# Four-layer hybrid on one core: the end of layer 0 image by image, and a new order of work ahead of layer 3's recurrence

## The chip, the cores and the metric

The kernel runs on one core of a Trainium2 chip. Its time is device microseconds for one execution, from the start of the program to its end. Five engines take part: TensorE (PE, matmuls; its weight loads are shown apart as PEld), VectorE (DVE), ScalarE (ACT), GpSimd (POOL) and SyncE (SP, which here only issues transfers). Each works through its own queue in order, and an instruction at the head of a queue that waits holds back what stands behind it. All arithmetic is fp32. In the trace an fp32 matmul leaves two rows; the text calls such a row a record.

## What is computed

Four layers act on x with 4 images, 256 channels and 32 x 32 positions (1024 tokens an image, 4096 in all). The parts that the change touches, cut from the reference:

```python
# end of layer 0: gate, root-mean-square norm, projection, excitation
y = y * silu(z)
y = y * rsqrt(mean(y * y, axis=-1, keepdims=True) + EPS) * rms_w
out = einsum('bld,ed->ble', y, out_w)
out_img = out.reshape(b, h, w, c).transpose(0, 3, 1, 2)
pooled = mean(out_img, axis=(2, 3))
hdn = relu(pooled @ se1_w.T + se1_b)
attn = sigmoid(hdn @ se2_w.T + se2_b)
x = x + out_img * attn[:, :, None, None]
# layer 3, attention (feature is the layer norm of the tokens t)
QK = einsum('bnd,kde->bkne', feature, W_qk) + b_qk[None, :, None, :]
value = einsum('bnd,de->bne', feature, W_v) + b_v
query, key = QK[:, 0], QK[:, 1]
lam = einsum('bnd,bne->bde', softmax(key, axis=1), value)
mean = mean(lam, axis=(0, 2)); var = var(lam, axis=(0, 2))
bn = (lam - mean) * rsqrt(var + BN_EPS) * gamma + beta
t = t + einsum('bnd,bde->bne', query, bn)
# layer 3, recurrence over the 1024 tokens, again on a layer norm of t
i, f, o = sigmoid(x_t @ U + h @ V + b)   # each with its own U, V, b
g = tanh(x_t @ U_c + h @ V_c + b_c)
c_new = h * c + i * g
h = o * tanh(c_new)
```

(In the recurrence the cell takes h * c, so the gate f is not needed, and the kernel computes three gates of 256 columns.) Layer 0 is a Mamba-like scan ahead of the lines shown, layer 1 a non-local block whose 1x1 products run over channels, layer 2 softmax attention and a mixture of eight experts, two for each token.

## The kernel before

Sizes: P = 128 partitions, C = 2 channel chunks of 128, D = 256, B = 4 images, W = 512 tokens a block, TPB = 4 token tiles a block, TPI = 8 tiles an image, NT = 32 tiles in all, BPI = 2 blocks an image. The program is unrolled; a scheduler places instructions by their data, and `_in_order` pins the order as written for the engines PE, DVE and ACT over a stretch of the program.

End of layer 0. `_scan` (L376) goes through 8 steps of tokens and in each through the 4 images: transposes and products on TensorE, an exponential on ScalarE, masking and sums on VectorE, and at the end of each tile the gate, which writes the gated rows `zs` (L436). When all 32 tiles are there, `_out_and_se` (L439) lets ScalarE square each and sum it (L449), takes a square root (L451) and a reciprocal (L452). Then for each of 8 blocks VectorE rescales four tiles by row (L459), TensorE transposes them into `pt` (L463), VectorE copies these to `yT` times `rms_w` (L464), TensorE multiplies by `w_out` into `po` (L470), and ScalarE copies that to `o` and sums it for the mean (L473). After the last block come the mean (L478), two small products with a relu (L484, L486) and, for each chunk, a third product (L489), the sigmoid `att` (L491) and four updates of x (L493). Layer 1 starts with 1x1 products over x by halves (L535). ScalarE's transfer queue loads weights: those of layer 2 behind the last sigmoid here.

`_rsqrt` (L971) is 1/sqrt by an integer first guess and four Newton steps of three VectorE operations (L990 to L994); the recurrence has a copy of it (L1517 to L1539).

Layer 3, attention (`_layer3_attention`, L1247). The experts' outputs lie in DRAM as two rows for each token. For each image and each half of it, SP loads both as `y_in` (L1282; three buffers, each freed by the addition), GpSimd adds the two (L1285), VectorE adds them to the tokens (L1287) and takes statistics (L1291, L1292). For the image follow `_rsqrt`, a shift (L1297) and eight normalised `rows` by ScalarE (L1302); TensorE transposes these into channels (L1268) and VectorE copies them to `u` (L1273). Then the keys (L1318), their copy, maximum and exponential (L1323 to L1333), transposes of these (L1343, copied at L1345 as `kt`) and of u (L1347, L1353), values (L1357) and `lam` (L1361). BatchNorm over lam follows for each chunk (L621 to L627, with a square root at L625) and an affine pass in two operations (L1377, L1378). lam is then multiplied by the query weights for every image: `p_q` (L1384), copied by ScalarE to `lam_q` (L1389), and with the query bias `p_b` (L1394), copied to `add_col` (L1398).

Layer 3, recurrence (`_layer3_lstm`, L1401). It starts with loads of `b_l`, `w_u` and `w_v` on ScalarE's queue and small constants (L1429 to L1443). `ahead(n)` is a generator that makes what batch n of 128 tokens an image needs: `attended(n)` multiplies u by `lam_q` (L1464) and adds it to x (L1458); `input_gates(n)` takes means (L1501), centred rows (L1487), squares (L1493), variances (L1511), 1/sqrt, a product that spreads it over rows (L1545), products with `w_u` (L1560) and gates `xg` (L1571). It yields after each instruction or so: False after a product, True after one of the small operations on VectorE. For n = 0 all of it runs ahead of the recurrence; for n = 1 to 7 one part is taken in each step of the batch before:

```python
        for _ in ahead(0):
            pass
        start = len(nc.cur_bb.bb.instructions)
        inputs(0)
        for t in range(L):
```

Its products share two PSUM buffers named `beside`. A step is: the gates' inputs (L1607), 48 products of the hidden state (L1616), transposes on VectorE (L1645), activations (L1646, L1659), the cell's scan (L1652) and the new hidden state (L1661), which is stored over x's old place. Sums to the output (`added`, L1585, L1586) follow batch by batch.

## Time and profile before

| what | value | from |
|---|---|---|
| median of 3 runs | 3514.43 us (3514.23 to 3514.61) | times |
| profiled execution | 3514.67 us | times |
| span of that execution | 3512.7 us | page |
| mean granted clock of TensorE | 0.969 | times |
| last gated row of the scan ends | 295.4 us | timeline |
| layer 1's first products end | 372.2 us | timeline |
| last expert row scattered | 1386.6 us | timeline |
| last lam summed | 1528.2 us | timeline |
| first product of the hidden state | 1582.9 us | timeline |

The span is the profiled execution's time between its first and its last instruction on the device; the 2.0 us between it and the execution's time lie around it. Times of the trace count from the span's start. The page's slices are 3512.7 / 40 = 87.8 us each. A group's line in the timeline reads: start in us, busy time, engine, line, operation, output<-inputs, shapes and count; in square brackets the idle time ahead of it and what ended that. A group's busy time is the sum over its instructions, which need not follow each other without gaps. In the chain of waits a line reads: time, length, engine, what, line.

### The profile page before, as it was taken

How to read it: one execution, taken by the hardware profiler on the slowest of the kernel's cores; microseconds unless marked ns; L12 is line 12 of the kernel's file. 1: busy time of each engine (PE TensorE's matmuls, PEld its weight loads, DVE VectorE, ACT ScalarE, POOL GpSimd, SP SyncE). 2: the span in 40 equal slices, each digit the busy share in tenths (PEclk: the TensorE clock that was granted, in tenths of full speed). 3: DMA queues.
4: the chain of work that ended last, by engine and by line, in shares of the span. 5: the costliest groups of instructions: out<-in, count | busy, mean ns of one | idle time of the engine just before them, and what ended most of it. 6: DMA issues, size and time to landing. Idle time of an engine off the chain costs nothing.

```text
span 3512.7 us, 146893 instructions
## 1 busy us (share of the span) xinstructions
PE 3227.6 (92%) x65412; PEld 2536.4 (72%) x65412; DVE 2016.5 (57%) x8382; ACT 1245.0 (35%) x5047; POOL 416.3 (12%) x498
## 2 busy tenths in 40 slices
PE   7786899998999997789999999999999999999888
PEld 4464344447788886468888888888888888888776
DVE  5795534452211111747777776777777777767666
ACT  4623222223222222413334344343343343433333
POOL 0182001122433332100000000000000000000000
PEclk9898899999999999899999999999999999999999
DMA  1290001115556554100000000000000000000000
GB/s 67 80 303 5 9 0 37 37 50 197 195 189 219 208 190 165 60 2 4 4 11 4 5 10 4 4 10 4 6 9 5 10 4 5 10 4 5 10 4 10
DMA packets 79355, 189.31 MB, mean 54 GB/s; under 512 B 6592, under 2 KB 64256, under 8 KB 73728
## 3 DMA queue, kind: packets, MB, share of 16 engines
q0 software_dynamic: 16176, 116.06, 9.0%
q1 hardware_dynamic: 60624, 59.12, 5.7%
q8 instruction: 511, 8.37, 1.0%
q10 hardware_dynamic: 1920, 4.74, 0.4%
q14 instruction: 124, 1.02, 0.1%
HBM read 118.88 MB, written 61.02 MB: 51 GB/s over the span
## 4 chain that ended last, share of the span: by engine, by line
PE 41%; DVE 9%; ACT 4%; issue 2%; ACTq 0%; DVEq 0%
PE p_c L1616 11%; DVE turned L1645 7%; PE p_c L1607 7%; PE p_i L1607 4%; PE p_o L1607 4%; PE p_i L1616 4%; PE p_o L1616 4%; PE beside L1560 4%; ACT a_o L1646 2%; DVE x L1661 2%; ACT th L1659 2%; PE beside L1464 1%; PE beside L1501 0%; PE var L1511 0%; PE p_q L1384 0%
## 5 line engine op out<-in xcount | busy, mean ns | idle before, releaser
L1646 ACT ACTIVATE add<-turned 128x8 f32<-128x8 f32 x1024 | 214.3, 209 | 1027.5 <-DVE turned L1645 1027.5
L1616 PE MATMUL p_c<-w_v,x 128*4 128x64 f32 x16368 | 416.0, 219 | 72.8 <-DVE x L1661 71.0
L1607 PE MATMUL p_c<-xg,shift 128*128 128x64 f32 x2048 | 445.7, 299 | 0.0
L1616 PE MATMUL p_o<-w_v,x 128*4 128x64 f32 x16368 | 416.6, 219 | 0.1
L1616 PE MATMUL p_i<-w_v,x 128*4 128x64 f32 x16368 | 416.5, 219 | 0.0
L1607 PE MATMUL p_i<-xg,shift 128*128 128x64 f32 x2048 | 406.8, 280 | 0.0
L1645 DVE STREAM_TRANSPOSE turned<-p_c 128x64 f32<-128x64 f32 x1024 | 255.9, 250 | 257.1 <-PE p_c L1616 226.7
L1607 PE MATMUL p_o<-xg,shift 128*128 128x64 f32 x2048 | 396.0, 275 | 0.0
L1607 PEld LDWEIGHTS p_c<-xg,shift 128*128 128x128 f32 x2048 | 304.7, 188 | 117.6 <-issue 0.3
L1616 PEld LDWEIGHTS p_c<-w_v,x 128*4 128x4 f32 x16368 | 227.2, 85 | 196.3 <-DVE x L1661 121.2
L1661 DVE TENSOR_TENSOR x<-a_o,th 128x8 f32<-128x8 f32 x1024 | 171.9, 168 | 245.4 <-ACT th L1659 245.4
L1607 PEld LDWEIGHTS p_o<-xg,shift 128*128 128x128 f32 x2048 | 310.9, 192 | 0.3
L1607 PEld LDWEIGHTS p_i<-xg,shift 128*128 128x128 f32 x2048 | 304.8, 188 | 0.4 <-issue 0.3
L1187 PE MATMUL ph<-uT,w 128*128 128x256 f32 x1248 | 284.6, 386 | 20.8 <-DVE uT L1172 20.7
L1191 ACT ACTIVATE hT<-ph,w 128x256 f32<-128x256 f32 x312 | 147.9, 474 | 395.2 <-PE ph L1187 394.8
L1187 PEld LDWEIGHTS ph<-uT,w 128*128 128x128 f32 x1248 | 240.4, 194 | 58.2 <-DVE uT L1172 24.6
L1201 PE MATMUL po<-w,hT 128*128 128x256 f32 x1248 | 282.1, 379 | 0.0
L1616 PEld LDWEIGHTS p_o<-w_v,x 128*4 128x4 f32 x16368 | 281.2, 87 | 0.3 <-issue 0.3
L1616 PEld LDWEIGHTS p_i<-w_v,x 128*4 128x4 f32 x16368 | 281.2, 87 | 0.3
L1645 DVE STREAM_TRANSPOSE turned<-p_i 128x64 f32<-128x64 f32 x1024 | 271.6, 265 | 0.7 <-PE p_i L1607 0.3
L1645 DVE STREAM_TRANSPOSE turned<-p_o 128x64 f32<-128x64 f32 x1024 | 256.0, 250 | 0.3 <-PE p_o L1616 0.3
L1201 PEld LDWEIGHTS po<-w,hT 128*128 128x128 f32 x1248 | 234.0, 190 | 30.2
(437 smaller groups left out, 4395.4 us busy)
## 6 DMA issues: line engine op xcount, KB each, us to landing
sorted<-zeros SPq DMA_DIRECT2D x32, 1032.0 KB, 14.4
y_in<-results SPq DMA_DIRECT2D x16, 512.0 KB, 5.3
x<-in_x_dram SPq DMA_DIRECT2D x8, 512.0 KB, 8.7
tokens<-rows SPq DMA_DIRECT2D x4, 1024.0 KB, 4.7
x<-tokens SPq DMA_DIRECT2D x8, 512.0 KB, 4.2
out_dram<-x_l SPq DMA_DIRECT2D x64, 64.0 KB, 1.7
results<-y,place POOLq DMA_INDIRECT x78, 4.4
w_l<-in_w_l_dram ACTq DMA_DIRECT2D x1, 1092.0 KB, 11.4
```

Of the source, the lines that this page charges most:

```text
L1187: nc.tensor.matmul(ph, w1[:, k, bass.ts(n, P)], uT[:, k, :], start=k == 0, stop=k == C - 1,)
L1191: nc.scalar.activation(hT[:, n, :], ph, AF.Gelu, bias=b1[:, n : n + 1])
L1201: nc.tensor.matmul(po, hT[:, n, bass.ts(a, P)], w2[:, n, :], start=n == 0, stop=n == NHC - 1,)
L1464: nc.tensor.matmul(p, lam[:, k, b, bass.ts(m, P)], u_l3[:, k, b * L + n * SB : b * L + (n + 1) * SB], start=k == 0, stop=k == C - 1,)
L1560: nc.tensor.matmul(p[bass.ts(i, R), :], rows[:, k, bass.ts(g, R)], w_u[:, k, at : at + GQ // GC], start=k == 0, stop=k == C - 1, tile_posi ...
L1607: nc.tensor.matmul(p[:, :H], shift[:, row * B : row * B + P], xg[n][:, g, bass.ts(i, H)], start=True, stop=t == 0,)
L1616: nc.tensor.matmul(p[R * i : R * i + B, :H], hs[:, t - 1, bass.ts(k, B)], w_v[:, k, i * GQ + g * H : i * GQ + (g + 1) * H], start=False, s ...
L1645: nc.vector.transpose(zt.rearrange("p c w -> p (c w)"), pz[g][:, :H])
L1646: nc.scalar.activation(dst.rearrange("p (c b) -> p c b", c=C), zt[:, :, :B], f)
L1659: nc.scalar.activation(th, cell[:, :, 1], AF.Tanh)
L1661: nc.vector.tensor_mul(h, a_o, th)
```

## The change

It has five parts.

First, the end of layer 0. The square of each gated tile is issued in `_scan` right behind the gate, into column c*B + b (token step c, image b). `_out_and_se` multiplies `rms_w` into the projection's weights once (`wo`), takes 1/sqrt by `_rsqrt` on VectorE, first for the 28 columns of the first seven steps and then for the last four, and goes image by image. For an image it rescales eight tiles, in turn on VectorE and ScalarE, transposes them, and lets ScalarE copy them to `yT` and sum them there. The mean over tokens is taken of yT, ahead of the projection, and goes through the projection as one column: `pooled`, `p1` and `p2` are products with one column each, in the fixed order on TensorE between the four `project(m, i)`. The projection stays in four PSUM banks, and x is updated from there in four operations an image.

Second, `_rsqrt` and the recurrence's copy of it take three Newton steps.

Third, the attention of layer 3. The two expert rows are added by VectorE one after the other, GpSimd adds nothing. Image 0 is normalised half by half, with PE, DVE and ACT in the order written for this stretch, and the additions of images 1 to 3 are put behind image 0's last copy to u (`later`, an order on VectorE without a semaphore).

Fourth, `_lstm_constants`: the loads of `b_l` and the small constants are issued ahead of the attention instead of behind it.

Fifth, lam's products. A fourth block of `w_l3` holds the query weights the other way round, and the attention ends with `q`, the queries of the first 128 tokens of each image. BatchNorm's affine pass is one operation with a scale and an offset; a square root with an output named `none`, which nothing reads, is issued ahead of BatchNorm. `attended(0)` multiplies `q` by the normalised lam itself. The products that were `p_q` and `p_b` become `queries()`, a generator of eight groups of eight records; `ahead(0)` takes a group from it at given parts, five among the products behind attended(0) and the others at every fourth small operation, with TensorE's order fixed up to the last group.

```diff
-NW = {"w_l0": 260 + 512 + 256 + 64, "w_l2": 768 + 8, "w_l3": 768, "w_u": 768, "w_v": 768}
+NW = {"w_l0": 260 + 512 + 256 + 64, "w_l2": 768 + 8, "w_l3": 1024, "w_u": 768, "w_v": 768}
...
+                sq = pool.tile([P, D], F32, name="sq")
+                nc.scalar.activation(sq, zs[:, n, :], AF.Square, accum_out=ss[:, c * B + b : c * B + b + 1])
...
+        ps = ctx.enter_context(tc.tile_pool(name="out_ps", bufs=3, space=PSUM))
...
+        wo = keep.tile([P, C, D], F32, name="wo")
+        for k in range(C):
+            nc.vector.tensor_scalar_mul(
+                wo[:, k, :], w_out[:, k, :], s.col["rms_w"][:, k : k + 1]
+            )
+        for t in (slice(0, NT - B), slice(NT - B, NT)):
+            nc.vector.tensor_scalar_mul(ms[:, t], ss[:, t], 1.0 / D)
+            for _ in _rsqrt(s, pool, rstd[:, t], ms[:, t]):
+                pass
+        for b in range(B):
+            for i in range(BPI):
+                for j in range(i * TPB, (i + 1) * TPB):
+                    n = b * TPI + j
+                    r = rstd[:, j * B + b : j * B + b + 1]
+                    if j % 2:
+                        nc.scalar.mul(y[:, n, :], y[:, n, :], r)
+                    else:
+                        nc.vector.tensor_scalar_mul(y[:, n, :], y[:, n, :], r)
+                for k in range(C):
+                    pt = ps.tile([P, TPB, P], F32, name="pt")
+                    for j in range(TPB):
+                        nc.tensor.transpose(
+                            pt[:, j, :], y[:, b * TPI + i * TPB + j, bass.ts(k, P)], s.ident
+                        )
+                    nc.scalar.activation(
+                        yT[:, k, bass.ts(i, W)], pt.rearrange("p j q -> p (j q)"), AF.Identity,
+                        accum_out=part[:, k, i : i + 1],
+                    )
+            mean = pool.tile([P, C], F32, name="mean")
+            nc.vector.tensor_reduce(mean, part, AX.X, ALU.add)
+            nc.vector.tensor_scalar_mul(mean, mean, 1.0 / L)
+            pooled, p1, p2 = small[:, b, :C], small[:NSE, b, C : C + 1], small[:, b, C + 1 :]
+            def project(m, i):
+                for k in range(C):
+                    nc.tensor.matmul(
+                        o[m][i], wo[:, k, bass.ts(m, P)], yT[:, k, bass.ts(i, W)],
+                        start=k == 0, stop=k == C - 1,
+                    )
+            start = len(nc.cur_bb.bb.instructions)
+            project(0, 0)
+            for m in range(C):
+                for k in range(C):
+                    nc.tensor.matmul(
+                        pooled[:, m : m + 1], wo[:, k, bass.ts(m, P)], mean[:, k : k + 1],
+                        start=k == 0, stop=k == C - 1,
+                    )
+            pooled_s = pool.tile([P, C], F32, name="pooled")
+            nc.vector.tensor_copy(pooled_s, pooled)
+            project(0, 1)
             for k in range(C):
+                nc.tensor.matmul(
+                    p1, w_se1[:, k, :], pooled_s[:, k : k + 1], start=k == 0, stop=k == C - 1
+                )
+            hdn = pool.tile([NSE, 1], F32, name="hdn")
+            nc.vector.tensor_scalar(hdn, p1, s.col["se1_b"][:NSE], 0.0, ALU.add, ALU.max)
+            project(1, 0)
+            for m in range(C):
+                nc.tensor.matmul(
+                    p2[:, m : m + 1], se2[:, bass.ts(m, P)], hdn, start=True, stop=True
+                )
+            project(1, 1)
+            _in_order(s, start, (mybir.EngineType.PE,))
...
             for m in range(C):
+                for i in range(BPI):
+                    xs = s.x[:, m, b, bass.ts(i, W)]
+                    nc.vector.scalar_tensor_tensor(
+                        xs, o[m][i], att[:, m : m + 1], xs, ALU.mult, ALU.add
+                    )
...
-    for _ in range(4):
+    for _ in range(3):
...
+    wq_t, wk, wv, wq = (w[:, :, i * D : (i + 1) * D] for i in range(4))
...
+            ahead = None
+            def later(held):
+                if ahead is not None:
+                    tc.add_manual_dep(
+                        held.ins, ahead.ins.name,
+                        mybir.DependencyInfo(
+                            mybir.DependencyClass.NoSync, mybir.DependencyReason.DATA
+                        ),
+                        reason="the first image leads",
+                    )
             for b in range(B):
+                start = len(nc.cur_bb.bb.instructions)
                 mv = pool.tile([P, TPI, 2], F32, name="mv")
...
+                def normalise(at, n):
+                    t = slice(at, at + n)
+                    for _ in _rsqrt(s, pool, rstd[:, t], mv[:, t, 1]):
+                        pass
+                    nc.vector.scalar_tensor_tensor(
+                        shift[:, t], mv[:, t, 0], -1.0, rstd[:, t], ALU.mult, ALU.mult
+                    )
+                    for j in range(at, at + n):
+                        nc.scalar.activation(
+                            rows[:, j, :], s.xr[:, b * TPI + j, :], AF.Identity,
+                            bias=shift[:, j : j + 1], scale=rstd[:, j : j + 1],
+                        )
                 for g in range(G):
                     i = b * G + g
                     y = yp.tile([P, 2, TPB, D], F32, name="y_in")
...
-                    nc.gpsimd.tensor_add(y[:, 0], y[:, 0], y[:, 1])
                     xr = s.xr[:, bass.ts(i, TPB), :]
-                    nc.vector.tensor_add(xr, xr, y[:, 0])
+                    for k in range(2):
+                        later(nc.vector.tensor_add(xr, xr, y[:, k]))
...
+                    if b == 0:
+                        normalise(g * TPB, TPB)
+                if b == 0:
+                    _in_order(s, start)
+                else:
+                    normalise(0, TPI)
                 for g in range(G):
                     for c in range(C):
-                        by_channel(
+                        done = by_channel(
                             u[:, c, b * L + g * W : b * L + (g + 1) * W],
                             lambda j: rows[:, g * TPB + j, bass.ts(c, P)], nc.vector,
                         )
+                if b == 0:
+                    ahead = done
...
+            for m in range(C):
+                p = ps.tile([P, B, W // B], F32, name="p_mm")
+                for k in range(C):
+                    nc.tensor.matmul(
+                        p, wq[:, k, bass.ts(m, P)],
+                        u.rearrange("p c (b l) -> p c b l", b=B)[:, k, :, : W // B],
+                        start=k == 0, stop=k == C - 1,
+                    )
+                nc.scalar.activation(
+                    q[:, m, :], p.rearrange("p b l -> p (b l)"), AF.Identity,
+                    bias=s.col["b_qk"][:, m : m + 1],
+                )
+            nc.scalar.activation(pool.tile([P, C], F32, name="none"), total, AF.Sqrt)
...
+            off = pool.tile([P, 1], F32, name="off")
+            nc.vector.tensor_mul(off, mean, scale)
+            nc.vector.tensor_sub(off, s.col["beta"][:, m : m + 1], off)
+            nc.vector.tensor_scalar(v, v, scale, off, ALU.mult, ALU.add)
+    return wq_t
...
+        def queries():
+            for b in range(B):
+                for m in range(C):
+                    p = ps2.tile([P, D + 1], F32, name="beside")
+                    for k in range(C):
+                        nc.tensor.matmul(
+                            p[:, :D], wq[:, k, bass.ts(m, P)], lam[:, k, b, :],
+                            start=k == 0, stop=k == C - 1,
+                        )
+                    for k in range(C):
+                        nc.tensor.matmul(
+                            p[:, D:], lam[:, k, b, bass.ts(m, P)], s.col["b_qk"][:, k : k + 1],
+                            start=k == 0, stop=k == C - 1,
+                        )
+                    nc.scalar.copy(lam_q[:, m, b, :], p[:, :D])
+                    nc.scalar.copy(add_col[:, m, b : b + 1], p[:, D:])
+                    yield
         def attended(n):
             held = None
             def add(xs, p, col):
-                nc.vector.scalar_tensor_tensor(xs, p, col, xs, ALU.add, ALU.add)
+                if col is None:
+                    nc.vector.tensor_add(xs, xs, p)
+                else:
+                    nc.vector.scalar_tensor_tensor(xs, p, col, xs, ALU.add, ALU.add)
             for b in range(B):
                 for m in range(C):
                     p = ps2.tile([P, SB], F32, name="beside")
                     for k in range(C):
+                        if n == 0:
+                            lhs, rhs, col = lam, q[:, k, bass.ts(b, SB)], None
+                        else:
+                            lhs, col = lam_q, add_col[:, m, b : b + 1]
+                            rhs = u_l3[:, k, b * L + n * SB : b * L + (n + 1) * SB]
                         nc.tensor.matmul(
-                            p, lam[:, k, b, bass.ts(m, P)],
-                            u_l3[:, k, b * L + n * SB : b * L + (n + 1) * SB],
-                            start=k == 0, stop=k == C - 1,
+                            p, lhs[:, k, b, bass.ts(m, P)], rhs, start=k == 0, stop=k == C - 1
                         )
                         if k == 0 and held is not None:
                             add(*held)
                         yield False
-                    held = x[:, m, b, bass.ts(n, SB)], p, add_col[:, m, b : b + 1]
+                    held = x[:, m, b, bass.ts(n, SB)], p, col
...
-        for _ in ahead(0):
-            pass
+        start = len(nc.cur_bb.bb.instructions)
+        fill = queries()
+        first = 2 * C * B + 1
+        smalls = 0
+        for i, part in enumerate(ahead(0)):
+            smalls += bool(part)
+            if i in range(first + 1, first + 11, 2) or part and smalls % 4 == 1:
+                if next(fill, True) is None:
+                    end = len(nc.cur_bb.bb.instructions)
+        _in_order(s, start, (mybir.EngineType.PE,), end)
...
-        "w_l3": np.concatenate([l3["W_qk"][0].T, l3["W_qk"][1], l3["W_v"]], 1),
+        "w_l3": np.concatenate(
+            [l3["W_qk"][0].T, l3["W_qk"][1], l3["W_v"], l3["W_qk"][0]], 1
+        ),
```

`_lstm_constants` holds the lines of L1429 to L1443 unchanged. `_in_order` gains two arguments: the engines it acts on and where it ends.

## What the change will do to the time

> **What bounds the kernel now.** I read the page's busy table first, then the slices, then the chain of waits with the timeline around each edit. The page:
>
> ```profile
> PE 3227.6 (92%) x65412; PEld 2536.4 (72%) x65412; DVE 2016.5 (57%) x8382; ACT 1245.0 (35%) x5047; POOL 416.3 (12%) x498
> ...
> PE   7786899998999997789999999999999999999888
> ```
>
> TensorE (PE) is busy 92%, but slices 3 and 4 (0-based, 263 to 439 us) and 16 and 17 (1405 to 1581 us) fall to 6 to 8 tenths: the end of layer 0 and layer 3 ahead of its recurrence. The edits lie there. The end of layer 0, from the timeline:
>
> ```profile
> 308.42 1.28 ACT L451 ACT_TABLE_LOAD   x1
> ...
> 310.07 0.35 DVE L452 RECIPROCAL rstd<-rstd 128x32 f32<-128x32 f32 x1 [14.65 <-ACT rstd L451]
> ...
> 310.96 2.02 PE L463 MATMUL pt<-ident,zs 128*128 128x128 f32 x8 [16.98 <-DVE zs L459]
> ...
> 319.99 3.67 PE L470 MATMUL po<-yT,w_l 128*128 128x512 f32 x8 [0.50 <-DVE yT L464]
> ...
> 323.50 1.04 PE L463 MATMUL pt<-ident,zs 128*128 128x128 f32 x8
> ...
> 357.47 9.66 DVE L493 SCALAR_TENSOR_TENSOR x<-o,att,x 128x1024 f32<-128x1024 f32 x8 [0.71 <-ACT att L491]
> ...
> 358.90 13.79 PE L535 MATMUL p<-x,w 128*32 128x512 f32 x64 [1.03 <-DVE x L493]
> ```
>
> TensorE stands still for 17 us while ScalarE takes 32 squares, then runs eight blocks at a 5.04 us period (319.99 to 325.03), then is paced by the eight updates of x. Layer 3 up to the second image's keys:
>
> ```profile
> 1402.40 1.23 DVE L1287 TENSOR_TENSOR x<-x,y_in 128x1024 f32<-128x1024 f32 x1 [16.10 <-POOL y_in L1285]
> ...
> 1410.57 2.31 DVE L984 TENSOR_SCALAR rstd<-half 128x8 int32<-128x8 int32 x1
> ```
>
> ```profile
> 1423.03 2.17 PE L1268 MATMUL p_x<-ident,rows 128*128 128x128 f32 x8 [37.58 <-ACT rows L1302]
> ...
> 1429.30 6.52 PE L1318 MATMUL p_mm<-u_l,w_l 128*128 128x512 f32 x14
> ...
> 1457.06 3.17 PE L1318 MATMUL p_mm<-u_l,w_l 128*128 128x512 f32 x7
> ```
>
> A 128x8 operation takes 2.31 us while GpSimd adds (0.16 us elsewhere), and the first image's keys start at 1426.5. After 1460 TensorE is busy 19 of every 20 us, so only a lead there reaches the end. The chain of waits behind it:
>
> ```profile
> 1530.48 1.28 ACT L625
> ...
> 1534.24 9.34 PE p_q L1384 x16
> 1543.59 3.48 PE p_b L1394 x32
> ...
> 1549.12 4.78 PE beside L1464 x24
> ...
> 1563.15 0.59 PE var L1545 x2
> ...
> 1564.35 1.51 PE beside L1560 x32
> ```
>
> lam's products stand on the chain for 12.8 us. From 1584 to 3510 us the recurrence makes 1023 steps of 1.87 to 1.89 us, whether small work (as in the first 127 steps of a batch) or none (the last batch, no next gates) stands beside it.
>
> **The change part by part.** A "record" is a matmul row of the trace; an fp32 matmul makes two. The sum starts from the profiled execution, 3514.67 us (span 3512.7 and 2.0 around it), 0.24 above the median of 3514.43.
>
> Squares into the scan. The last gated row ends at 295.43 (L436, 295.00 + 0.43). Before, 15.5 us pass until the transposes at 310.96. In the changed order 28 squares stand among the scan's exponentials and four behind the last of them; three of those have their input by 295, so one is left, 0.4 + 0.19 + about 0.2 to signal = 0.8. Then VectorE does 19 Newton operations of 0.08 (independent) to 0.20 us (dependent; L990 to L994 at 1448 to 1452 stand 0.20 apart), about 3.1, and the first four rows are rescaled on two engines, 0.6. Two scalings of w_out (0.28 each, the L459 row's 1.93/7) come before: 0.6. Start 295.4 + 5.1 = 300.5, so -10.5. A square waits on ScalarE ahead of the next exponential, and behind that wait the masked product on VectorE: in steps 3 to 7 this may add 0.2 each, and later z's row ends (266.1) before the exponential it precedes starts (268.37). I take +0, bounds 0 and 28 x 0.6 = 17.
>
> Projections. For an image TensorE needs 16 transposes 2.08, 16 records of 512 at 3.51/8 = 7.0, 16 records with one column at 3.48/32 = 1.75, and about 0.4 of waits (yT's second copy, the mean): 11.2 against 2 x 5.04. The first image pays 1.5 for the clock (first eight records 5.51 against 3.67) and 1.0 for copies that share ScalarE with rescalings. VectorE's updates of x (0.65 each) and the sigmoids lie beside the next image's transposes; four banks and two images' order leave 2 us of slack. Uncovered they would cost 4 x 0.65 an image. Layer 1's products then run unpaced: the second half takes 369.05 to 372.2 = 3.2, two halves and the 0.9 between them 7.8 with pipeline. So 300.5 + 4 x 11.2 + 2.5 + 7.8 = 355.6 against 372.2: -16.6. Layer 1 waits on the weights' load for layer 2 no sooner than before (issued behind the last sigmoid, 4.2 to land); bound 0 to +2.
>
> One Newton step less. Three operations of 0.20: 0.6 each for images 0 and 1 at the start and for layer 1's gain, -1.8 in all; elsewhere beside TensorE. In the recurrence three small parts fewer in each of seven batches: 0, since steps with and without are alike; bounds -0.2 and +0.5 (21 x 0.02). Together with the above: -18.4.
>
> First image leads. GpSimd's eight additions (2.34 each) become eight more on VectorE (1.22). Nothing else stands on GpSimd there. y_in's loads on SP wait for buffers that VectorE's additions free; three buffers and a load every 3.3 us (GpSimd's starts 1400.03, 1403.40, 1406.39) keep them ahead. On ScalarE's queue w_l3's load grows from 768 to 1024 KB and four b_l loads (1.76 us of issue) go ahead of w_u and w_v: the first y_in, issued at 1393.74 beside them, lands perhaps 0.5 later. Then, one after the other: 1400.5, one addition 1.2 (the other came with the first load), four statistics 2.5, 14 operations at 0.195 = 2.75, so the first four rows at 1407; second half two additions 2.4, statistics 2.5 and two copies 1.4, Newton 2.75: 1416; rows, transposes, copies to 1419.7; six matmuls of key to 1425.3 against 1435.8, a lead of 10.5. It isn't kept: in VectorE's changed order image 1's four additions and image 2's four (8 x 1.2), their statistics and image 1's Newton steps stand between image 0's kt copies, and image 1's shift stands behind image 0's lam. Adding these rows from 1430.8: about 16 us of VectorE work, lam at 1447, shift 1447.8. Rows (0.5 each), copies and two additions more bring image 1's keys effectively to 1452.5 against 1457.06: -4.5. Bounds: 0 or +3 (clock low through the waits) and -10.5.
>
> lam's products in waits. BatchNorm: the table load (1.28) moves ahead of it; the affine pass becomes one (-0.75 for each half) against two small operations more. lam's second half is ready at 1534.05 instead of 1535.6; the new queries (8 records, 3.5) fit between 1528.4 and 1532. The first batch's products start at 1534.05 instead of 1546.92: -12.9. Constants (fold, mask, shift, 1.9) go to the idle time before 1400, so the batch ends at 1539.9 instead of 1554.3: -14.4. What comes back: eight query groups of 4 x 0.25 + 4 x 0.11 = 1.45, 11.6 in all, of which the means', squares' and Newton waits cover only part. In order: 4 means 1.7, queries 11.6, variances 1.9, waits for two PSUM buffers 1.2, the spread product 0.6: 1557 against 1563.75, the first xg one product later, and two w_u products that stood ahead of it now follow (1.0): at the recurrence -5.8. Bounds: 1.9 a group (the clock of p_q, 0.58 a record) gives -2; all groups hidden -12.
>
> Page against row: the Trainium skill, ScalarE: Activation LUTs, What ACT_TABLE_LOAD costs, gives a switch of tables 1.28 us and about 1.38 of drain, 2.66 in all. Here the load at 308.42 follows the last square's accumulator read (to 308.41) at once and the activation starts at 309.72, so no drain shows; by the page the two loads taken off the path would be worth 2.8 us more than my sum has.
>
> Sum: -18.4 - 4.5 - 5.8 = -28.7, so 3486.0; from the median 3485.7. I say 3486.
>
> **The rivals.**
> (A) Layer 3 gives nothing: the lead is absorbed before 1460 and the groups run at the low clock. For it: 0.79 granted clock between 1423 and 1447, VectorE 90% busy there. Against: the 12.8 us chain is really gone. 3514.7 - 18.4 = 3496.
> (B) Layer 3 gives all: -10.5 and -12. For it: TensorE waits while VectorE works. Against: VectorE's order. 3514.7 - 18.4 - 22.5 = 3474.
> (C) The squares stall the scan: 28 x 0.6 less the cover; with half of it, 8.4, the time is 3494; with all 3503. Against: VectorE is 95% busy from 200 to 295 us, the exponentials have slack.
> (D) Slower: the recurrence's step. lam_q lies at another address and a product's tile is wider; if a step of L1616 to L1663 grows by 28 ns or more (28.7/1023) everything is given back; at 35 ns 3521. Against: the order of a step is unchanged, and steps differ by 0.02 us at most.
> (E) The order does what it says but TensorE's clock makes each image of layer 0 2 us dearer: 3494.
>
> **How the numbers follow.** Forecast 0.55, A 0.15, B 0.11, C 0.09, E 0.05, D 0.03, something within 0.2% 0.02. This kernel's measurement tells about 0.2% (7 us) from no change. All but D and the last are over 7 us faster: faster 0.95, same 0.02, slower 0.03. The range takes the forecast's own 3479 to 3493 (terms of 4, 4 and 4 us off) and reaches to A and nearly to B: 3476 to 3499.
>
> **What would show it.** After: the first L463-like transposes near 300.5 and a gap of 6, not 17 us; images 11.2 apart; layer 1's products ending near 355; the first keys' end 10 us earlier relative to the last scatter, the second image's keys only 4.5; lam's first product 2.4 us behind lam's statistics; the recurrence 28.7 earlier with steps of 1.87. Wrong if the scan's rows stretch, if images are 13 apart, or if the groups hold the spread product longer than 17 us.

## The result, and the profile after

The changed kernel takes 3473.98 us (median of 4 runs, 3471.44 to 3474.85), before beside it 3514.33 (3510.33 to 3514.61): a ratio of 0.9887, 95% interval 0.9869 to 0.9904. Forecast were 3486 and a range of 3476 to 3499. The sign was right; the time lies 12 us below the forecast and 2 us below the range. The profiled execution took 3474.85 with a span of 3472.9.

The slices of the page (counted from 0): TensorE (PE) is at 8 in slices 3 and 4 now, where it had 6 and 8. The dip ahead of the recurrence is one slice shorter: before it had 7, 7 and 8 in slices 15 to 17, now 7 and 8 in 15 and 16.

```profile
PE 3231.7 (93%) x65492; PEld 2543.0 (73%) x65492; DVE 2003.3 (58%) x8361; ACT 1253.7 (36%) x5081; POOL 399.3 (11%) x490
...
PE   7788899989999997899999999999999999999888
```

The end of layer 0, from the timeline: the last gate, the only square behind it, the last Newton operation on the 28 columns, the transposes of the four images, layer 1's products.

```profile
291.66 0.42 DVE L439 TENSOR_TENSOR zs<-zs,y 128x256 f32<-128x256 f32 x1
...
292.17 0.42 ACT L441 ACTIVATE sq<-zs 128x256 f32<-128x256 f32 x1 [2.97 <-DVE ms L465]
...
295.23 0.26 DVE L1036 SCALAR_TENSOR_TENSOR rstd<-e,rstd 128x28 f32<-128x28 f32 x2
...
295.95 3.65 PE L482 MATMUL pt<-ident,zs 128*128 128x128 f32 x16 [5.60 <-ACT zs L476]
...
308.86 2.03 PE L482 MATMUL pt<-ident,zs 128*128 128x128 f32 x16
...
319.76 2.10 PE L482 MATMUL pt<-ident,zs 128*128 128x128 f32 x16
...
330.73 2.10 PE L482 MATMUL pt<-ident,zs 128*128 128x128 f32 x16
...
341.79 7.07 PE L577 MATMUL p<-x,w 128*32 128x512 f32 x64
```

TensorE stands still for 5.6 us, not 17. The transposes of the images start 12.9, 10.9 and 11.0 us apart, layer 1's products 11.1 behind the last, and these take 7.1 us where they took 13.8.

Layer 3 up to image 1's shift, and the stretch up to the first product of the hidden state (called the first hidden product from here on). Line 1518.77 is one of the eight query groups, line 1526.05 the product that spreads 1/sqrt over rows, called the spread product:

```profile
1371.87 1.23 DVE L1385 TENSOR_TENSOR x<-x,y_in 128x1024 f32<-128x1024 f32 x1 [9.80 <-DMA y_in<-results]
...
1384.02 3.75 PE L1411 MATMUL p_mm<-u_l,w_l 128*128 128x512 f32 x4 [0.69 <-issue]
...
1419.45 0.92 DVE L1454 SCALAR_TENSOR_TENSOR lam<-p_mm,total,rows 128x256 f32<-128x256 f32 x2
1420.28 0.15 DVE L1366 SCALAR_TENSOR_TENSOR shift<-mv,rstd 128x8 f32<-128x8 f32 x1
...
1503.54 4.18 PE L1568 MATMUL beside<-q,lam 128*128 128x128 f32 x30 [1.04 <-DVE lam L1486]
...
1518.77 1.99 PE L1536 MATMUL beside<-lam,w_l 128*128 128x256 f32 x4
...
1526.05 0.37 PE L1647 MATMUL var<-spread,fold 128*128 128x16 f32 x2
...
1543.93 0.41 PE L1718 MATMUL p_c<-w_v,x 128*4 128x64 f32 x16
```

The same place before, the last lam and the first batch's products:

```profile
1528.20 0.92 DVE L1361 SCALAR_TENSOR_TENSOR lam<-p_mm,total,rows 128x256 f32<-128x256 f32 x2 [1.22 <-PE p_mm L1357]
...
1546.92 1.14 PE L1464 MATMUL beside<-u_l,lam_q 128*128 128x128 f32 x8
```

Image 0's keys start 23.3 us behind the last expert scatter (1360.7) instead of 39.9, but image 1's shift stands right behind image 0's lam, as forecast. Thirty of the first batch's 32 records start 5.4 us behind the last lam (1498.1), where before they started 18.3 behind. (The last lam is the second of its pair, 0.4 behind the start of the pair's line.)

The table gives each stage against before's profile, in us, worked out from the starts of rows: when the scan starts (by its second gated row); its length up to the last gate; from there to the last of layer 1's first products; layer 2's experts, first product to last scatter; from there to the last key product of layer 3, called the lead; from the last lam to the first hidden product; the recurrence. Minus is faster than before. What lies between these columns makes -0.9 to +2.0 each. The rows e1 to e16 are the experiments of the next section.

| kernel | scan starts | scan | end of layer 0 | experts | lead | to first hidden | recurrence |
|---|---|---|---|---|---|---|---|
| forecast | -1.2 | 0 | -16.6 | 0 | -4.5 | -5.8 | 0 |
| after | -1.7 | -1.7 | -20.5 | -3.0 | -4.6 | -8.5 | -0.8 |
| e5, after again | -1.1 | +0.4 | -21.2 | -2.3 | -5.5 | -10.2 | -0.8 |
| e13, after again | -1.6 | -1.7 | -20.4 | -2.7 | -5.2 | -11.9 | -2.9 |
| e1, layer 0 alone | +0.4 | -1.0 | -19.6 | +0.3 | +0.1 | +1.3 | -2.6 |
| e2, Newton alone | -1.3 | +0.7 | -0.6 | +1.3 | -0.7 | -0.6 | -2.5 |
| e3, layer 3 alone | +0.6 | +0.6 | -0.2 | +3.6 | -0.4 | -8.2 | -0.9 |
| e4, squares behind | -1.6 | -0.6 | -10.1 | -0.8 | -3.8 | -10.2 | -0.8 |
| e6, no queries | -2.3 | -0.9 | -19.8 | -3.2 | -4.1 | -12.8 | -0.9 |
| e7, first group | -2.2 | -1.8 | -21.2 | -1.9 | -2.6 | -25.0 | +11.8 |
| e8, hold more | -1.5 | -0.1 | -21.0 | -2.7 | -7.6 | -8.5 | -4.0 |
| e9, four steps | 0.0 | +0.4 | -19.5 | +3.3 | -0.3 | -8.2 | -2.5 |
| e10, queries first | -1.6 | -1.6 | -20.4 | +2.0 | -4.7 | -7.4 | -1.5 |
| e11, hold and first group | -1.4 | -1.7 | -20.3 | +2.4 | -9.0 | -21.6 | -2.5 |
| e12, the same and a sigmoid | -1.6 | -1.6 | -20.5 | +1.1 | -9.2 | -20.0 | +0.1 |
| e14, four in layer 2 | -1.4 | -1.7 | -20.3 | -2.2 | -5.5 | -10.2 | -0.7 |
| e15, four in layer 3 | -1.9 | -1.7 | -20.5 | -1.6 | -2.1 | -8.5 | -0.4 |
| e16, e11 again | -2.1 | +0.1 | -19.9 | -1.3 | -8.9 | -20.0 | -0.8 |

Two things scatter: the experts move by -3.2 to +3.6 without an edit to their products, and the median of before itself was 3512 to 3519 beside these runs. The two go together, by the session in which kernels were timed. In e1 to e4 (before at 3517.0) the experts are at -0.8 to +3.6, in e5 to e8 (3512.0) at -3.2 to -1.9, in e9 to e12 (3519.0) at +1.1 to +3.3, in e13 to e16 (3513.4) at -2.7 to -1.3. So totals are compared as ratios to the before beside them, and differences in the experts' column count only within a session.

### The profile page after: what moved, and what is told of

Read it like the earlier page. It is cut to its first block, busy times and chain, and to the rows that moved or that the text cites. A ratio compares the mean times of both kernels' runs of the same rounds, so it can differ in the third digit from the quotient of the medians.

```text
span 3472.9 us, 147036 instructions
## 1 busy us (share of the span) xinstructions
PE 3231.7 (93%) x65492; PEld 2543.0 (73%) x65492; DVE 2003.3 (58%) x8361; ACT 1253.7 (36%) x5081; POOL 399.3 (11%) x490
## 4 chain that ended last, share of the span: by engine, by line
PE 44%; DVE 10%; ACT 4%; issue 2%; DMA 0%; ACTq 0%; SPq 0%; DVEq 0%
PE p_c L1718 11%; DVE turned L1757 7%; PE p_c L1709 7%; PE p_i L1709 5%; PE p_o L1718 4%; PE p_o L1709 4%; PE p_i L1718 4%; PE beside L1662 4%; ACT a_o L1758 2%; DVE x L1773 2%; ACT th L1771 2%; PE beside L1568 1%; PE p_u L1440 1%; PE p_mm L1411 1%; PE beside L1603 1%
```

## The experiments

### One part alone

e1 has only the diff of layer 0's end (squares, images, `_rsqrt` of the gates) on the kernel before; e3 only that of layer 3, with `range(4)` kept in both; e2 is one token, twice:

```diff
-    for _ in range(4):
+    for _ in range(3):
```

> Layer 0's end as after, everything else (four Newton steps, layer 3) as before. By the stages of the changed kernel's trace: the last gated row 0 to 1.7 us earlier than before, layer 1's first products end 21 to 22 us earlier (23.8 less the 1.7 that the scan starts earlier there), total 3514.4 - 21 = 3493. By my prediction's terms: 16.6 earlier, 3498. Rival: the 3 us that layer 2 gained in the changed kernel come with layer 0's earlier end, then 3490; if they are chance, this kernel's layer 2 is 0 to 3 us off either way.

> Three Newton steps in place of four, nothing else changed (one step less of the iteration everywhere). By my prediction: 0.6 each for images 0 and 1 and for layer 1's gain, 1.8, and one more for image 0 of layer 3, so 3512. If the 3.3 us by which the changed kernel's scan ends earlier belong to this edit (start and phase of the scan) and not to the squares, the last gated row is 3.3 earlier here and the total 3510; if 1.7 are the start and the rest the squares, it is 1.7 earlier.

> Layer 3 as after, layer 0's end as before, four Newton steps everywhere. By the changed kernel's trace layer 3 is worth 13.1 us up to the first step and 0.75 in the recurrence; with 3 Newton chains of 0.6 on its path added back, 12: 3502. By my prediction's terms, 4.5 + 5.8 less 1.8 for Newton: 3506. Rival: layer 2 gains 3 us here too, though nothing ahead of it changed, then its gain is chance and the total 3499.

Measured beside before at 3517.0: e1 3498.07 (0.9953, 0.9936 to 0.9969), e2 3512.01 (0.9988, 0.9978 to 0.9997), e3 3509.87 (0.9981, 0.9972 to 0.9991). The three add to 0.78% (each known to 0.1 or 0.2), the change has 1.13%. By stages layer 0's end adds up (-19.6, -0.6 and -0.2 against -20.5). The stretch to the first hidden product makes -7.5 in all (+1.3, -0.6 and -8.2) against -8.5 to -11.9 in three profiles of after. The lead doesn't add up: layer 3 alone keeps nothing of it (-0.4), and Newton alone hardly moves it (-0.7), while together they make -4.6 to -5.5. VectorE's order in e3, at image 0's lam:

```profile
1450.56 0.92 DVE L1413 SCALAR_TENSOR_TENSOR lam<-p_mm,total,rows 128x256 f32<-128x256 f32 x2
1451.39 0.16 DVE L991 TENSOR_TENSOR e<-rstd,v 128x8 f32<-128x8 f32 x1
...
1451.53 1.22 DVE L1344 TENSOR_TENSOR x<-x,y_in 128x1024 f32<-128x1024 f32 x1
1452.67 0.16 DVE L993 TENSOR_TENSOR e<-e,rstd 128x8 f32<-128x8 f32 x1
...
1452.82 1.22 DVE L1344 TENSOR_TENSOR x<-x,y_in 128x1024 f32<-128x1024 f32 x1
1453.96 0.16 DVE L995 SCALAR_TENSOR_TENSOR rstd<-e,rstd 128x8 f32<-128x8 f32 x1
...
1454.18 0.16 DVE L1325 SCALAR_TENSOR_TENSOR shift<-mv,rstd 128x8 f32<-128x8 f32 x1
```

The fourth step's three operations come behind lam with two additions of 1.22 between them, and the shift 3.6 us behind lam's start where the changed kernel has it 0.8 behind.

### The squares

e4 moves the square out of the scan and issues all 32 in `_out_and_se`:

```diff
-                nc.scalar.activation(sq, zs[:, n, :], AF.Square, accum_out=ss[:, c * B + b : c * B + b + 1])
...
+        for c in range(TPI):
+            for b in range(B):
+                sq = pool.tile([P, D], F32, name="sq")
+                nc.scalar.activation(
+                    sq, y[:, b * TPI + c, :], AF.Square, accum_out=ss[:, c * B + b : c * B + b + 1]
+                )
```

> The changed kernel with the 32 squares behind the scan, all else as after. If squares cost the scan nothing: the last gated row at 292.1 as after, 31 more squares of 0.42 ahead of the first transposes, 13.0, total 3474 + 13 = 3487. If they stalled the scan (my rival C, up to 17 us less cover), the scan ends earlier by that and the total lies between 3474 and 3487. If the scan even runs faster with squares in it, the last gate is later, 293.7, and the total 3488.6.

3487.61 (0.9928, 0.9911 to 0.9944). The end of layer 0 gets 10.4 us longer than in after: half of what that part gives. (By the ratios the total is 14 to 17 longer; the two profiles differ by 11.9, and what is not in this stage lies in columns that move by chance as well.) The scan's length is -0.6 here, -1.8 to +0.4 in fourteen profiles with squares in it and -0.6 to +0.7 in four without. So the squares cost the scan nothing that shows, and the -1.7 of after comes and goes (+0.4 in e5, the same kernel).

### The queries

e6 leaves `queries()` out, so its batches from the second on multiply by a constant; e10 issues all of it first (`for _ in queries(): pass` ahead of `ahead(0)`). Both fix TensorE's order over the whole stretch. e5 is after once more.

> The changed kernel once more, beside the kernels that edit it. 40 us below before; its stages show what repeats: layer 2 gained 3.0 us in its first profile and lies between -0.8 and +3.6 in four other kernels, so 0 +- 3 here if that is chance and -3 if it belongs to the change; the last lam 4.6 us earlier against the last scatter and the first hidden product 8.5 against the last lam if these are the change's.

> The changed kernel without the eight groups of query products, which are left out (the batches from the second on then multiply by a constant). This measures what the groups cost ahead of the recurrence. My prediction's terms: 11.6 us of groups, of which the waits cover about 5, so 6 to 7 faster. By the changed kernel's trace: five groups of 1.53 stand ahead of the variances and three of 2.5 between these and the spread product, whose inputs were ready at 1521.6 and which ran at 1526.05; without them the variances come after four means of some 1.2 us, 1512.5, and the spread product at 1517.3: 8.7 faster. If waits cover them: under 2.

> The changed kernel with all eight groups of queries ahead of the first batch's products, not in waits between. Eight groups at 1.53 are 12.2 on the path; interleaved they cost the first hidden product 4.3 and the end 2.4 (run without queries). So 8 to 10 slower, 3479 to 3481, if the places in the waits are what hides them. Rival: the waits that they leave open lower TensorE's granted clock, as in the run without queries, and it costs more than 10. A second: the groups stand on the path wherever they are, and it costs under 4.

e5 3470.79 (0.9881, 0.9864 to 0.9897), e6 3468.37 (0.9874, 0.9857 to 0.9890), e10 3483.16 (0.9902, 0.9886 to 0.9919; before beside it 3519). By stages, the eight groups (1.31 us each at the full clock in e13, 10.5 in all) cost the first hidden product 1.0 to 4.3 (e6 against the three profiles of after), and to put them first costs 1.1 to 4.5 more, not 8 to 10; the totals would allow 5 to 7, with intervals of 6 on each. The columns of the next view: stretch, its length, busy time of PE, PEld, DVE, ACT and POOL with counts, then the granted clock (1.00 is full speed), the DMA's share and GB/s. First e6, then after:

```profile
1507.00:1514.00 7.00, 6.63 (x31) 6.38 (x32) 2.34 (x15) 0.00 (x0) 0.00 (x0) 0.53 0.00 0
1520.00:1527.00 7.00, 6.40 (x114) 5.46 (x118) 2.83 (x12) 2.14 (x3) 0.00 (x0) 0.53 0.01 2
```

```profile
1507.70:1517.00 9.30, 9.29 (x58) 8.11 (x57) 2.92 (x9) 3.40 (x12) 0.00 (x0) 1.00 0.01 2
1517.00:1526.40 9.40, 9.40 (x48) 8.30 (x51) 2.19 (x14) 1.48 (x7) 0.00 (x0) 0.64 0.00 0
1526.40:1532.70 6.30, 6.20 (x179) 4.82 (x182) 4.45 (x17) 3.48 (x8) 0.00 (x0) 1.00 0.01 3
```

Without the groups TensorE's clock is halved in two stretches of 6.8 us, one over the first batch's products and the means, the other over the first gates; after has one.

What such a low stretch costs here can be read off, because many profiles share the work. From the last lam to the end of the spread product they take 24.9 us without a low stretch in between (e7, e13), 26.6 with one of 3.4 us (e4, e5, e11, e14) and 28.2 or 28.3 with one of 6.8 (after, e8, e12, e15, e16): 1.7 for each 3.4. From there to the first hidden product, where all 16 groups of gates stand in between, it is 17.5 in the nine profiles without a low stretch (after, e3, e4, e5, e8, e9, e13, e14, e15) and 18.6 to 20.8 in the five with one (before, e1, e2, e6, e10). The ends of the first of these stretches in e13:

```profile
1498.78 0.91 DVE L1454 SCALAR_TENSOR_TENSOR lam<-p_mm,total,rows 128x256 f32<-128x256 f32 x2 [1.22 <-PE p_mm L1450]
...
1523.77 0.38 PE L1647 MATMUL var<-spread,fold 128*128 128x16 f32 x2
```

e6 takes 21.7 to its spread product with 6.8 us at half clock, so some 18.3 at full clock, an estimate by the same 1.7 for each 3.4. That is 6.6 less than e13: at an equal clock the groups cost 6 to 7 us, and the waits hide some 4 of their 10.5. (e10, where no wait hides them, has its spread product 3.4 later than e13; a low stretch that begins 3.7 us ahead of it may be part of that.) The clock took the rest back in e6: about 3.4 ahead of the spread product by this estimate, and 2.3 behind it (19.8 instead of 17.5). So the groups look as cheap as 1.0 to 4.3 for two reasons: waits cover part of them, and without them more of the time ran at half clock.

### Holding more, and starting the recurrence earlier

e8 holds images 2 and 3 behind image 1's shift. e7 starts the recurrence behind the first of the 16 groups of gates and chains the other parts in front of the next batch's, one each step. e11 is both, and three more groups inside step 0; e12 adds a sigmoid that nothing reads to it; e16 is e11 again. The edits of e8, e7 and e11, shortened and in this order:

```diff
                 else:
-                    normalise(0, TPI)
+                    last = normalise(0, TPI)   # returns the shift
+                    if b == 1:
+                        ahead = last
...
-        for i, part in enumerate(ahead(0)):
+        zero = ahead(0)
+        for i in range(first + 39):
+            part = next(zero)
...
-                parts = ahead(n + 1) if (n + 1) * SB < L else iter(())
+                if n == 0:
+                    parts, part = behind(zero), None   # zero, then ahead(1) to ahead(7)
...
-            if i == SB - 1:
-                for _ in parts:
-                    pass
+            if t == 0:
+                for _ in range(12):
+                    next(parts)
```

> The changed kernel, with the additions of images 2 and 3 held behind image 1's shift instead of image 0's last copy to u. My prediction held that the first image's lead is not kept because VectorE's order puts image 2's additions and statistics ahead of image 1's shift: then the shift (1420.3) comes about 8 earlier, image 1's keys with it, and the last lam 4 to 8 earlier. Rival: TensorE is the limit there, with 1.3 us idle at 1420; then under 2. A second rival: images 2 and 3 get late in turn (their shifts stood 15 to 20 us ahead of use), and it is slower.

> The changed kernel, but the recurrence starts behind the first of the 16 groups of gates (8 tokens each); the other 60 parts go one per step ahead of the next batch's parts, which lag. The chain of waits gives 16 groups 0.98 each ahead of the first hidden product at 1543.9, though its first gates were there at 1526.96 and its first state at 1531.9. If a part beside a step is free, as my prediction read from steps with and without, the first hidden product comes 12.0 earlier and so does the end. Rival: steps of the last batch, which had none, get 0.02 to 0.4 longer, or the parts wait in the steps: then less than 12, down to 0.

e8: 3469.94 (0.9885, 0.9868 to 0.9901) beside e5's 0.9881: no difference in the total that can be told, though the lead is -7.6 instead of -4.6 to -5.5. The shift came earlier and image 1's rows with it (48.9 us behind the last scatter, 58.9 in e5), but only 2 to 3 us of these 10 reach the last key. e11, e12 and e16 have the same hold and a lead of -8.9 to -9.2, so 3.4 to 4.6 more than the three profiles of after; e8's profile has a low stretch of 6.8 us behind image 1's keys, the three others one of 3.4. From 1440 to 1480 TensorE is busy 39 of 40 us in e8 and in e5 from 1442 to 1482 alike, so there it is the limit.

e7: 3465.46 (0.9863, 0.9846 to 0.9879), its runs spread from 3459 to 3473. The profiled execution is the longest of them, 3473.1, with a mean granted clock of 0.971; the two shortest have 0.974 and 0.975. In it the first hidden product came 13 to 16 us earlier than in after, and the recurrence gave 13 to 15 of it back:

```profile
1520.00:1528.00 8.00, 7.92 (x88) 7.15 (x87) 3.70 (x20) 3.29 (x9) 0.00 (x0) 1.00 0.00 0
1528.00:1530.00 2.00, 0.77 (x34) 0.49 (x36) 0.53 (x3) 1.24 (x4) 0.00 (x0) 1.00 0.04 8
1530.00:1560.00 30.00, 30.00 (x600) 26.80 (x586) 12.63 (x63) 6.46 (x39) 0.00 (x0) 0.51 0.01 2
```

TensorE had little to do for 2 us while the first state was made, and then half the clock for 30.7; nine steps took 3.2 us each instead of 1.87.

> Images 2 and 3 held behind image 1's shift, and the recurrence started behind the first group of gates, now with 12 more parts (three groups, 2.9 us of products) issued inside step 0, where TensorE stood idle for 1.2 us ahead of a stretch of 30.7 us at half clock in the first-group run. If that idle time brought the low clock: 2.5 from the hold and 11.8 less the 0.5 that the parts delay step 0, so 3471 - 14 = 3457 in every run. If the first steps bring it themselves: 3462 to 3470, with the spread of 14 us that the first-group run had.

> As the run before, with one more activation (sigmoid of one column, which nothing reads) behind BatchNorm. ScalarE loads tables twice in step 0, 1.28 each, one of them in the chain of the first state (1529.77 in the changed kernel). If the added activation brings the table that holds both functions: 1.3 to 2.6 faster than the run before. If copies and squares in between load another table, or the load delays lam_q's copies: 0 to 1.3 slower.

e11 3466.89 (0.9854, 0.9838 to 0.9870; before beside it 3519.0), e12 3466.60 (0.9856, 0.9840 to 0.9873). The times of e11 lie in the range expected for the case that the first steps bring the low clock themselves, but before was 7 us slower beside it than beside e7; the profiles decide. In e11, e12 and e16 no low stretch falls between the first hidden product and the program's last few us, and a part in a step is then free: the mean step of the first batch is 1.88 us in e16, as it is in before and after from the second batch on. That the work inside step 0 keeps the clock up rests on one profile without it (e7) and three with it; the hold, which e7 lacks, lies over 100 us ahead. In e16, the same kernel as e11:

```profile
1527.00:1531.00 4.00, 3.67 (x111) 2.71 (x103) 2.75 (x11) 2.18 (x5) 0.00 (x0) 1.00 0.01 4
1531.00:1560.00 29.00, 29.00 (x948) 24.62 (x944) 20.20 (x99) 11.32 (x61) 0.00 (x0) 1.00 0.02 5
```

The sigmoid makes no difference that can be told. In e11 two table loads of 1.28 us stand between the spread product and the first hidden product, in e12 none (one stands at 1503.9), and both take 6.1 us there: the loads were not on the path.

### Where the fourth Newton step sits

e9 is after with `range(4)` in both places; e14 and e15 take four steps in one place each, layer 2's norm and the norm of images 1 to 3 of layer 3.

> The changed kernel with four Newton steps everywhere: what the one step less is worth inside the change. By my prediction's term: 1.8 ahead of layer 2 and 0.6 in layer 3, so 3471 + 2.4 = 3473.4. By the traces so far more: the same three operations less also change the order of instructions in layer 2 (kernels with four steps took 0 to 3.6 more there than before, the changed kernel 2.0 to 3.2 less) and put image 1's shift right behind image 0's lam, where with four steps two additions of 1.2 stood between (layer 3 alone, four steps: the last lam 0.4 earlier, the changed kernel 4.6 to 5.5). Then 1.7 + 2.6 to 6 + 4.5 = 9 to 12 more: 3480 to 3483.

> The changed kernel once more, as the reference on the same chip for the three kernels beside it: 40 to 42 us below before.

> The changed kernel with four Newton steps in layer 2's norm alone, which gives layer 2 the order of instructions that it had before, on all engines. If the order is what layer 2 gained: from the first expert product to the last scatter 1.5 to 3 longer than in the changed kernel beside it, and the total 1.5 to 3 longer. If that stage only differs by chance: within 1 of it.

> The changed kernel with four Newton steps in the norm of images 1 to 3 of layer 3 alone. By the rows, three operations of 0.16 to 0.2: 0.6 and no more, if they stand alone. By VectorE's order with four steps (seen in layer 3 alone): the last operations of image 1 come behind image 0's lam with two additions of 1.22 between them, the shift 2.8 later behind lam, the last lam 3 to 4 later, and the total 3 to 4 longer.

> The version with images 2 and 3 held behind image 1's shift and the recurrence started behind the first group of gates, beside the changed kernel: 11 to 14 faster than it, 0.3 to 0.4%.

e9 3490.32 (0.9920, 0.9904 to 0.9937), 11 to 14 us above after by the ratios: 1.1 to 1.7 at the start of the scan, 4 to 5 in the lead, and the rest in columns that move by chance as well (the experts at +3.3, in a session where the kernels beside it have +1.1 to +2.4). In one session, beside before at 3513.36: e13, after, 3473.98 (0.9889, 0.9874 to 0.9904); e14 3474.71 (0.9890, 0.9875 to 0.9905); e15 3481.72 (0.9910, 0.9895 to 0.9925); e16 3459.33 (0.9843, 0.9830 to 0.9856).

e14 gives layer 2 its old order of instructions back and its experts take 0.6 us more than in e13, so the order is not what they gained: that theory fell. e15 loses 3.1 us of the lead against e13, by the same two additions as in e3 (the rest of the 7.7 between their medians lies in columns where profiles of one kernel differ too):

```profile
1419.34 0.92 DVE L1454 SCALAR_TENSOR_TENSOR lam<-p_mm,total,rows 128x256 f32<-128x256 f32 x2
1420.17 0.16 DVE L1032 TENSOR_TENSOR e<-rstd,v 128x8 f32<-128x8 f32 x1
...
1420.32 1.22 DVE L1385 TENSOR_TENSOR x<-x,y_in 128x1024 f32<-128x1024 f32 x1
...
1421.61 1.22 DVE L1385 TENSOR_TENSOR x<-x,y_in 128x1024 f32<-128x1024 f32 x1
...
1422.96 0.16 DVE L1366 SCALAR_TENSOR_TENSOR shift<-mv,rstd 128x8 f32<-128x8 f32 x1
```

Image 1's shift stands 3.6 us behind the start of image 0's lam here, 2.8 more than in after. Around the start of image 1's keys e15 has a low stretch of 6.8 us where e13 has one of 3.4, which may be part of the 3.1.

e16 beats both kernels: 14.6 us below the changed one beside it (3473.98 less 3459.33), 54 below before. Expected were 11 to 14 below the changed one.

## Why the prediction was right or wrong

The sum had -28.7, the two profiles differ by 39.8 in span: 11.1 more. The mechanisms of the forecast are in the trace, and no rival's took their place. The step that failed is the size of two of its terms. The end of layer 0 was put at -16.6 and measures -20.5. In the term for lam's products the first gates were taken over at 19.2 us, with 1.0 added, and measure 17.5. These make 3.9 and 2.7 of the 11.1. The rest lies where the sum had nothing: 3.0 in the experts, 1.7 in the scan's length (which e5, the same kernel, does not repeat) with 0.5 more at its start, 0.8 in the recurrence, 0.1 in the lead, and 1.5 the other way between the layers.

**Squares into the scan, -10.5.** The restart was put 5.1 us behind the end of the last gate; it is 3.9 (295.95 less 292.07). The two scalings of w_out, 0.6 in the sum, ran between the last rows of the scan, and the Newton operations of the two parts ran interleaved. e4 gives 10.4 for the squares. The "+0" for the scan held, with bounds far too wide.

**Projections.** 47.3 was forecast for the four images, 45.8 measured; 7.8 for layer 1's products, 7.1 measured. The old end was set at 372.2, in the table ahead of the prediction too; by its own line it is 372.7 (358.90 + 13.79). With 1.2 at the restart these make the 3.9.

**One Newton step less, -1.8.** Before layer 2 this was near: 1.1 to 1.7 at the scan's start, where 1.2 had been put, and 0.9 between layer 1's products and the experts in e2, where 0.6 had been put. "Elsewhere beside TensorE" was wrong: on image 1 of layer 3 the step is worth 3.1 (e15). It lay inside my term for the lead, whose sum had counted VectorE's changed order with three steps, so the total didn't suffer.

**First image leads, -4.5.** 4.6 to 5.5 measured in three profiles, for the reason given: image 1's shift stands behind image 0's lam. (Kernels that differ from after only elsewhere have 2.6 to 5.5; e7, the lowest, starts image 0's keys 25.2 us behind the scatter.) The other limit was close: with the shift 10 us earlier only 2 to 5 more come through (e8, e11, e12, e16). What the term did not see is how thin it was: with one step more everywhere 0.3 or 0.4 of it is left (e9, e3).

**lam's products in waits, -5.8.** The spread product was put 28.4 us behind the last lam and came 28.3 behind (1526.4 less 1498.1). That is luck: the sum had no low clock in it, while after's profile has 6.8 us of it there, and without it the product comes 24.9 behind (e13). Two sizes in it were too large: the first batch's products at 5.9 us, taken from rows of which 3.4 us ran at half clock (1549.0 to 1552.4), where they take 4.1 in after; and a query group at 1.45, where it takes 1.31 at the full clock. The miss that shows lies behind it, at the first gates: 17.5 us instead of 20.2. The first 5.7 of the 19.2 us that were taken over ran at half clock, and I had not looked at the clock of that stretch. Before, then after:

```profile
1563.20:1569.50 6.30, 5.67 (x98) 4.78 (x102) 2.60 (x10) 0.79 (x2) 0.00 (x0) 0.50 0.00 1
```

```profile
1526.40:1532.70 6.30, 6.20 (x179) 4.82 (x182) 4.45 (x17) 3.48 (x8) 0.00 (x0) 1.00 0.01 3
```

In other profiles of the same kernel the stage to the first hidden product was -10.2 and -11.9: its low stretch was 3.4 us long or missing, where after's own was 6.8.

**What was left out.** The experts came out 3.0 faster and the recurrence 0.8, both put at nothing. Of the edits the Newton step is the one that changes their instructions, and it is worth nothing there that can be told: 0.6 in the experts (e14), and in the recurrence four steps (e9) have -2.5 where after's three profiles have -0.8 to -2.9. The experts' column goes by the session and not by the edits. No profile of before was taken in the sessions of e1 to e16, so how much of the 3.0 is the change's, and why sessions differ, stays open. A range for a kernel of 3500 us that allowed 4 us for each of three terms and nothing for all that stays the same was too narrow: 3 us more below would have held the time.

**The rivals.** A fell: layer 3 gave 13, not nothing. B's 3474 is the time that came, but not by its mechanism: the lead was -4.6 and not -10.5, and the groups were not hidden. C fell with the scan's lengths. D fell: the median step is 1.874 us before and after. E fell: the images are 11 apart, and the first, 12.9, took less than the 13.7 that it had been given.

## What to carry to other kernels

Look at the granted clock of a stretch before its time is taken over: a row at half clock can be cheaper in the changed kernel (17.5 us instead of 19.2 for the first gates), and a stage from which work is removed can lose part of the gain to a lower clock (e6). Compare a stage between kernels at an equal clock. Where a scheduler orders an engine, three small operations cost what comes to stand between them (in e15 3.1 us for 0.5 us of work), so a term that rests on an order is as thin as that order. In a long kernel the unchanged part needs its own place in the range.

## What the runs showed of the hardware

The low clock comes in stretches of a multiple of 3.41 us (3.4, 6.8, 10.2, 30.7) at half speed, all but the one that the end of the program cuts off; added up from the trace's own records of the clock they make 218 us before and 175 after. The Trainium skill, TensorE: Matmul & The Clock Gate, What's actually happening, has this window and gives one idle window as what lowers the clock and one busy window as what restores it. The length agrees with the traces. The conditions do not quite agree: in e7 some 1.2 us without work in a stretch of 2.0 were followed by 30.7 us at half clock although TensorE's records fill that whole time, and in after the clock fell at 1518.9 behind 9.3 us in which its records are 9.29 busy. What the gate counts as busy the runs do not show.

The recurrence has two paces between profiles of the same code, a median step of 1.871 (e13) or 1.874 us (after, e5): 1023 steps make 3 us of it. Its cause wasn't tried.
